# Pairwise bilinear interaction: x in a ring of five tiles, loads in pairs, four stores a tile, products in place

## The chip, the cores and the metric

One Trainium2 chip, one core of it. The time is microseconds of the device for one execution of the whole kernel. Engines: PE (matrix), DVE (vector), ACT (scalar), POOL (GpSimd), SP (issues transfers). Sixteen DMA engines move data between HBM and the on-chip buffer; transfers are issued here from the queues of SP, ACT and POOL.

## The reference

```python
# inputs: (4096, 32, 64) f32;  W: (496, 64, 64) f32
idx_i, idx_j = np.triu_indices(32, k=1)            # 496 pairs i < j
vidots = jnp.einsum('bpd,pde->bpe', inputs[:, idx_i, :], W)
y = vidots * inputs[:, idx_j, :]                   # (4096, 496, 64) f32
```

For each row b of the batch and each pair (i, j), the 64 numbers of field i are multiplied by the pair's own 64 x 64 matrix, and the result is multiplied element by element with field j. x is 33.6 MB, W 8.1 MB and the output 520.1 MB.

## The kernel before, in words

The 4096 rows are 16 blocks of 256; a block is two tiles of 128 rows (row 2p + k of a block is partition p of its tile k), so there are 32 tiles. Field i of a tile has a run of pairs (i, i+1) to (i, 31), which begins at pair p0[i]; the runs get shorter, from 31 pairs to 1.

**Weights.** W comes in four chunks of rows (`cuts`, `wrows`). Each is loaded with a pair per partition (`load_w`, L133), put in another order by a copy (`order_w`, L139, into a buffer of `tpool`), transposed by PE in eight blocks (`turn_w`, L148) and copied from PSUM to its place in wT (L151). A chunk takes four such rounds. The first chunk is done before the main loop; the rounds of the other three are placed at steps of the main loop by the lists `orders` and `turns`.

**x.** A block is loaded into one of two buffers of `xpool` (`new_x`, `load_x`, L81). For each run of 8 fields of a tile, PE transposes four pairs of fields (`turn_x`, L159) and ACT copies the result to an xT buffer in three pieces (L163 to L165; four buffers, `xtpool`). This is done AHEAD = 6 steps before the first use.

**Steps.** A step is one field i and up to 16 of its pairs. PE multiplies into one of four PSUM buffers (L259, one matmul for each half of the 64 outputs). Then either DVE multiplies the PSUM result with x_j into the output buffer `ot` (L279); or, for the first 16 pairs of i = 1, 3, ..., 13 (`aside`), ACT copies PSUM out (L276) and POOL multiplies (L277). In the first three tiles ACT copies straight into `ot` and POOL works in place; in later tiles ACT's copy goes to a `tmp` buffer of `tpool`.

**Stores.** The 496 pairs of a tile are divided by `bounds` into five groups of 90 to 105 pairs. Each group fills one of three `ot` buffers (`opool`) and is stored by one transfer from SP (L284); the very first group is stored in two parts. A row of a group, 23,040 to 26,880 bytes, is contiguous in HBM, so a store is 128 packets, eight for each DMA engine.

**Order.** The first three tiles (`LEAD`) go through the groups together: group 0 of tiles 0, 1, 2, then group 1, and so on, while the weights are still being prepared. After that it is tile by tile. Blocks 0 and 1 and the weights are loaded by SP at the start. Later blocks are loaded one at a time while the block before is used: blk + 1 is issued at step LATE = 6 of the first tile of blk (block 2 at that step of tile 3). Blocks 2, 3, 4, 6, 8, 10 and 12 are issued from ACT's queue, as one transfer of 16 KB a partition. Blocks 5, 7, 9, 11, 13, 14 and 15 (`fifteen`) are issued from POOL's queue (`load_fifteen`): 120 partitions over fifteen of the DMA engines, so that one is skipped; a tiny transfer (`turn_engines`, L97) that moves on the engine at which POOL's next transfer begins; and the 8 partitions left over in two transfers, each with half of the fields of both tiles, in packets of 4 KB (L105). In SBUF these blocks have a gap of 16 numbers between their two tiles.

The scheduler of the tile framework adds the semaphores. The order on an engine is the order in the program, and a pool's buffer is reused when its readers are done.

Of the kernel before, what the change touches and what calls it, by code (L numbers as in the profile page):

```python
# [8 lines left out]
F32 = mybir.dt.float32  # L9
# [3 lines left out]
def kernel(  # L13
# [15 lines left out]

    nc = tc.nc  # L30

    B, F, D = x.shape
    P = 128
    NB = 2
    assert 2 * D == P and B % (NB * P) == 0
    NBLK = B // (NB * P)
    NP = F * (F - 1) // 2
    E2 = D // 2
    BANK = 512
    CH = BANK // E2  # L40
    RUN = 8
    p0 = [i * (F - 1) - i * (i - 1) // 2 for i in range(F)]


    bounds = [0, p0[3], p0[6] + CH, p0[11], p0[17], NP]
    groups = list(zip(bounds[:-1], bounds[1:]))
    cap = max(b - a for a, b in groups)

    aside = (1, 3, 5, 7, 9, 11, 13)

    cuts = [0, P, 2 * P, NP - P, NP]
    wrows = list(zip(cuts[:-1], cuts[1:]))

    const = ctx.enter_context(tc.tile_pool(name="const", bufs=1))
    xpool = ctx.enter_context(tc.tile_pool(name="xpool", bufs=2))
    xtpool = ctx.enter_context(tc.tile_pool(name="xtpool", bufs=4))
    tpool = ctx.enter_context(tc.tile_pool(name="tpool", bufs=4))
    opool = ctx.enter_context(tc.tile_pool(name="opool", bufs=3))
    psum = ctx.enter_context(tc.tile_pool(name="psum", bufs=4, space=bass.MemoryType.PSUM))

    ident = const.tile([P, P], F32, tag="ident", name="ident")
    make_identity(nc, ident)

    xs = {}
# [4 lines left out]


    fifteen = (5, 7, 9, 11, 13, 14, 15)

    def new_x(blk: int):
        gap = 16 if blk in fifteen else 0
        wide = xpool.tile([P, NB * (F * D + 16)], F32, tag="xs", name=f"xs_{blk}")
        wide = wide[:, : NB * (F * D + gap)].rearrange("p (k n) -> p k n", k=NB)
        xs[blk] = wide[:, :, : F * D].rearrange("p k (f d) -> p k f d", d=D)

    def load_x(blk: int, eng, k0: int = 0, k1: int = NB):
        src = rows_of(x, blk).rearrange("(p k) f d -> p k f d", k=NB)  # L80
        eng.dma_start(out=xs[blk][:, k0:k1], in_=src[:, k0:k1])  # L81
# [4 lines left out]
    SWR = 120  # L86
# [13 lines left out]
    def load_fifteen(blk: int):  # L100
        rows = rows_of(x, blk).rearrange("(p k) f d -> p k f d", k=NB)
        dst = xs[blk]

        def part(ps: slice, fs: slice):
            tc.keep_in_program_order(nc.gpsimd.dma_start(out=dst[ps, :, fs, :], in_=rows[ps, :, fs, :]))  # L105

        part(slice(0, SWR), slice(0, F))
        turn_engines(1)
        for h in range(2):
            part(slice(SWR, P), slice(h * F // 2, (h + 1) * F // 2))  # L110


    wflat = w.rearrange("p d e -> p (d e)")
    raw, wT = {}, {}
    EU = 2 * BANK // P
    NU = E2 // EU


    def home_of(c: int, r: int):
        home, tag, n = (wrows[3][0], "w3", P) if c == 3 else (0, "w", 3 * P)  # L120
        if home not in wT:
            wT[home] = const.tile([P, n, E2], F32, tag=tag, name=f"wT_{home}")
        return wT[home][:, wrows[c][0] - home : wrows[c][0] - home + r, :]

    def load_w(c: int):

        a = wrows[c][0]
        if c == 2:
            raw[c] = home_of(c, P).rearrange("p r e -> p (r e)")
        else:  # L130
            pool, tag = (const, "w3") if c == 3 else (opool, "ot")
            raw[c] = pool.tile([P, D * D], F32, tag=tag, name=f"raw_{c}")
        nc.sync.dma_start(out=raw[c], in_=wflat[a : a + P])  # L133

    def order_w(c: int, k: int, copy):
        r = wrows[c][1] - wrows[c][0]
        rp = tpool.tile([P, EU, 2, D], F32, tag="tmp", name=f"rp_{c}_{k}")
        src = raw[c][:r, :].rearrange("p (d h e) -> p e h d", h=2, d=D)
        ins = copy(rp[:r], src[:, k * EU : (k + 1) * EU])  # L139
        if c > 0:  # L140
            tc.keep_in_program_order(ins)
        return rp

    def turn_w(c: int, k: int, rp, copy):
        r = wrows[c][1] - wrows[c][0]
        pt = psum.tile([P, EU, P], F32, tag="ps", name=f"ptw_{c}_{k}")
        for n in range(EU):
            nc.tensor.transpose(  # L148
                pt[:, n, :r], rp[:r, n].rearrange("p h d -> p (h d)"), ident[:r, :r]
            )  # L150
        copy(home_of(c, r)[:, :, k * EU : (k + 1) * EU], pt[:, :, :r].rearrange("p e r -> p r e"))  # L151

    def turn_x(blk: int, k: int, q: int, copy):


        pt = psum.tile([P, RUN // 2, P], F32, tag="ps", name=f"ptx_{blk}_{k}_{q}")
        for u in range(RUN // 2):
            f = q * RUN + 2 * u
            nc.tensor.transpose(  # L159
                pt[:, u, :], xs[blk][:, k, f : f + 2, :].rearrange("p f d -> p (f d)"), ident  # L160
            )
        xT = xtpool.tile([P, 2, RUN // 2, P], F32, tag="xT", name=f"xT_{blk}_{k}_{q}")
        copy(xT[:, 0], pt)  # L163
        copy(xT[D:, 1], pt[:D])  # L164
        copy(xT[:D, 1], pt[D:])  # L165
        return xT


    steps = [
        (g, i, c0, min(CH, F - 1 - i - c0))  # L170
        for i in range(F - 1)
        for c0 in range(0, F - 1 - i, CH)
        for g, (a, b) in enumerate(groups)
        if a <= p0[i] + c0 < b
    ]
    NS = len(steps)
    first = {}
    for s, (_, i, _, _) in enumerate(steps):
        first.setdefault(i, s)

    LEAD = 3
    NT = NBLK * NB
    sched = [
        (t, s) for g in range(len(groups)) for t in range(LEAD) for s in range(NS) if steps[s][0] == g
    ]
    sched += [(t, s) for t in range(LEAD, NT) for s in range(NS)]
    place = {ts: n for n, ts in enumerate(sched)}


    AHEAD = 6
    due: dict = {}
    for t in range(NT):
        for q in range(F // RUN):
            at = place[t, first[q * RUN]] - AHEAD
            due.setdefault(max(0, at), []).append(("x", t // NB, t % NB, q))
    for c, orders, turns in (
        (1, (2, 4, 8, 10), (4, 7, 12, 15)),
        (2, (16, 18, 25, 27), (30, 33, 36, 39)),  # L200
        (3, (46, 48, 50, 52), (56, 59, 62, 65)),
    ):
        for k in range(NU):
            due.setdefault(orders[k], []).append(("order", c, k))
            due.setdefault(turns[k], []).append(("turn", c, k))
    LATE = 6
    loads = {place[blk * NB, LATE]: blk + 1 for blk in range(2, NBLK - 1)}
    loads[place[LEAD, LATE]] = 2

    new_x(0)  # L210
# [4 lines left out]
    new_x(1)  # L215
# [5 lines left out]
    v, p, a = nc.vector.tensor_copy, nc.gpsimd.tensor_copy, nc.scalar.copy  # L221
    xT, rps = {}, {}
    xT[0, 0, 0] = turn_x(0, 0, 0, a)
    due[0] = [d for d in due[0] if d != ("x", 0, 0, 0)]
# [5 lines left out]
    ots = {}  # L230
    for s, (t, st) in enumerate(sched):
        blk, kt = divmod(t, NB)
        g, i, c0, m = steps[st]
        if s in loads:
            new_x(loads[s])
            if loads[s] in fifteen:
                load_fifteen(loads[s])
            else:
                load_x(loads[s], nc.scalar)
        for what, *args in due.get(s, ()):  # L240
# [4 lines left out]
            else:  # L245
                c, k = args
                rps[c, k] = order_w(c, k, ((v, v, p, v), (v, v, p, a))[k % 2][c])

        base, end = groups[g]
        pa = p0[i] + c0  # L250
        if pa == base:
            ots[t] = opool.tile([P, cap, D], F32, tag="ot", name=f"ot_{t}_{g}")
        ot = ots[t]
        ps = psum.tile([P, 2, CH, E2], F32, tag="ps", name=f"ps_{s}")
        for lo, hi in ((0, wrows[3][0]), wrows[3]):
            home, lo, hi = lo, max(pa, lo), min(pa + m, hi)
            if lo < hi:
                for h in range(2):
                    nc.tensor.matmul(  # L259
                        ps[:, h, lo - pa : hi - pa, :],  # L260
                        xT[blk, kt, i // RUN][h * D : (h + 1) * D, (i + h) % 2, i % RUN // 2, :],
                        wT[home][h * D : (h + 1) * D, lo - home : hi - home, :],
                        start=True,
                        stop=True,
                    )
# [4 lines left out]
        xj = xs[blk][:, kt, j : j + m, :].rearrange("p m (h e) -> p m h e", h=2)  # L270
        if i in aside and c0 == 0:

            tmp = dst
            if t >= LEAD:
                tmp = tpool.tile([P, CH, 2, E2], F32, tag="tmp", name=f"tmp_{s}")
            nc.scalar.copy(tmp, src)  # L276
            nc.gpsimd.tensor_mul(dst, tmp, xj)  # L277
        else:
            nc.vector.tensor_mul(dst, src, xj)  # L279

        ends = (p0[2], end) if s < NS and (t, g) == (0, 0) else (end,)
# [34 lines left out]
```

## Time and profile before

| | us |
|---|---|
| five executions, median (lowest to highest) | 1334.17 (1332.33 to 1335.5) |
| the profiled execution, its own time | 1335.4 |
| its span, first to last instruction | 1333.6 |
| PE busy, modelled | 1129.5 (85%) |
| DVE busy | 950.8 (71%) |
| POOL busy | 558.4 (42%) |
| ACT busy | 471.6 (35%) |
| DMA, mean of 16 engines | 9 tenths or more in all but one of 40 slices |
| TensorE clock granted | 0.956 |

How to read it: busy times are sums over the span for each engine, and they overlap. The page lists DMA queues with packets, bytes and the share of the sixteen DMA engines' time that their packets took; the records behind it have the start, size and duration of each packet. A wait "A <- B" is idle time of A that ended with B. A stretch is a window of the span with the busy time of each engine in it, the share of DMA time and GB/s.

### The profile page before, as it was taken

What the parts mean: (1) busy time and instruction counts of PE and PEld (TensorE: products, weight loads), DVE (VectorE), ACT (ScalarE), POOL (GpSimd) and SP (SyncE); (2) the same over time, 40 slices, a digit from 0 to 9 for tenths busy, and PEclk for the clock granted to TensorE, in tenths of its full rate; (3) what the DMA queues carried; (4) which work ended last, traced back from release to release, by engine and by line L of the source; (5) the groups of instructions that cost most, each with busy time, mean ns of one, the idle gap of its engine ahead of it and who ended that gap; (6) DMA issues with size and microseconds to landing.
All of it is one profiled execution on the core that took longest, in us unless ns stands there. A gap on an engine that the chain in (4) does not pass through costs nothing.

```text
span 1333.6 us, 16690 instructions
## 1 busy us (share of the span) xinstructions
PE 1129.5 (85%) x6656; PEld 599.2 (45%) x6656; DVE 950.8 (71%) x1258; ACT 471.6 (35%) x627; POOL 558.4 (42%) x264
## 2 busy tenths in 40 slices
PE   6989879878888888888888888898897988978894
PEld 3555434434444444444444444444444444434442
DVE  5878767767777776777767777676875767757784
ACT  4463323333333333233333333332333333333331
POOL 1752424444433445333453334542445443444441
PEclk9999999989999899999998989998998989989997
DMA  9999999999999999999999999999999999999998
GB/s 389 431 424 421 430 422 431 427 431 427 413 428 425 432 431 414 428 427 431 431 412 431 424 431 422 414 431 424 432 427 411 428 413 428 429 419 420 421 427 351
DMA packets 28143, 563.13 MB, mean 422 GB/s; under 512 B 3761, under 2 KB 3761, under 8 KB 4113
## 3 DMA queue, kind: packets, MB, share of 16 engines
q1 hardware_dynamic: 24192, 532.69, 94.0%
q0 software_dynamic: 2864, 14.70, 2.8%
q10 hardware_dynamic: 1008, 14.68, 2.6%
q8 instruction: 52, 0.85, 0.2%
q14 instruction: 27, 0.21, 0.0%
HBM read 41.94 MB, written 520.09 MB: 421 GB/s over the span
## 4 chain that ended last, share of the span: by engine, by line
DMA 61%; PE 16%; DVE 15%; POOL 3%; issue 2%; ACT 1%; DVEq 0%; SPq 0%; POOLq 0%; ACTq 0%
DMA out_dram<-ot 60%; PE ps L259 15%; DVE ot L279 14%; POOL ot L277 3%; PE ptx L159 1%; DMA xs<-in_r_inputs_dram 1%; DVE rp L139 0%; ACT tmp L276 0%; PE ptw L148 0%; DVEq L279 0%; POOL rp L139 0%; ACT ot L276 0%; SPq L133 0%; ACT xT L165 0%; ACT xT L163 0%
## 5 line engine op out<-in xcount | busy, mean ns | idle before, releaser
L279 DVE TENSOR_TENSOR ot<-ps,xs 128x1024 f32<-128x1024 f32 (+15 forms) x1248 | 935.9, 807 | 353.5 <-DMA out_dram<-ot 219.0
L259 PE MATMUL ps<-wT,xT 64*128 64x512 f32 (+12 forms) x6016 | 1039.6, 485 | 171.0 <-DVE ot L279 166.3
L259 PEld LDWEIGHTS ps<-wT,xT 64*128 64x128 f32 x6016 | 530.4, 194 | 620.9 <-DVE ot L279 384.2
L277 POOL TENSOR_TENSOR ot<-tmp,xs 128x1024 f32<-128x1024 f32 x203 | 479.2, 2361 | 697.6 <-ACT tmp L276 517.7
L276 ACT COPY tmp<-ps 128x1024 f32<-128x1024 f32 x203 | 205.5, 1012 | 471.6 <-PE ps L259 427.5
L163 ACT COPY xT<-ptx 128x512 f32<-128x512 f32 x128 | 75.0, 586 | 324.9 <-PE ptx L159 324.9
L159 PE MATMUL ptx<-ident,xs 128*128 128x128 f32 x512 | 84.4, 288 | 10.7 <-DMA xs<-in_r_inputs_dram 7.2
L159 PEld LDWEIGHTS ptx<-ident,xs 128*128 128x128 f32 x512 | 53.9, 141 | 82.8 <-DVE ot L279 58.0
L165 ACT COPY xT<-ptx 64x512 f32<-64x512 f32 x128 | 74.5, 582 | 1.6
L164 ACT COPY xT<-ptx 64x512 f32<-64x512 f32 x128 | 73.9, 577 | 1.5
L277 POOL TENSOR_TENSOR ot<-ot,xs 128x1024 f32<-128x1024 f32 x21 | 49.8, 2376 | 50.9 <-ACT ot L276 50.8
L276 ACT COPY ot<-ps 128x1024 f32<-128x1024 f32 x21 | 21.3, 1013 | 24.7 <-PE ps L259 15.0
L148 PE MATMUL ptw<-ident,rp 128*128 128x128 f32 (+1 forms) x128 | 17.7, 289 | 5.8 <-DVE rp L139 5.8
L139 DVE COPY rp<-raw 128x1024 f32<-128x1024 f32 x9 | 14.7, 1649 | 10.7 <-DMA raw<-in_L_rec_W_dram 10.7
L148 PEld LDWEIGHTS ptw<-ident,rp 128*128 128x128 f32 (+1 forms) x128 | 14.9, 150 | 13.8 <-DVE rp L139 5.2
L151 ACT COPY wT<-ptw 128x1024 f32<-128x1024 f32 (+1 forms) x15 | 14.8, 985 | 11.6 <-PE ptw L148 10.2
L105 POOL DMA_DIRECT2D xs<-in_r_inputs_dram x21 | 13.4, 637 | 0.0
L97 POOL DMA_DIRECT2D scratch<-in_r_inputs_dram x9 | 8.2, 911 | 0.3 <-issue 0.3
L139 POOL COPY rp<-wT 112x1024 f32<-112x1024 f32 x4 | 7.9, 1978 | 0.0
L139 ACT COPY rp<-raw 128x1024 f32<-128x1024 f32 x3 | 6.0, 1986 | 1.9 <-DMA raw<-in_L_rec_W_dram 1.9
L151 DVE COPY wT<-ptw 128x1024 f32<-128x1024 f32 x1 | 1.2, 1225 | 2.4 <-PE ptw L148 2.4
L163 ACT ACT_TABLE_LOAD x1 | 1.3, 1283 | 0.7 <-PEq L303 0.7
(6 smaller groups left out, 0.9 us busy)
## 6 DMA issues: line engine op xcount, KB each, us to landing
out_dram<-ot SPq DMA_DIRECT2D x64, 3360.0 KB, 16.3
out_dram<-ot SPq DMA_DIRECT2D x32, 3168.0 KB, 15.7
out_dram<-ot SPq DMA_DIRECT2D x32, 3104.0 KB, 17.0
out_dram<-ot SPq DMA_DIRECT2D x31, 2880.0 KB, 17.2
xs<-in_r_inputs_dram ACTq DMA_DIRECT2D x7, 2048.0 KB, 18.7
xs<-in_r_inputs_dram POOLq DMA_DIRECT2D x7, 1920.0 KB, 24.9
raw<-in_L_rec_W_dram SPq DMA_DIRECT2D x3, 2048.0 KB, 13.9
xs<-in_r_inputs_dram SPq DMA_DIRECT2D x2, 1024.0 KB, 10.4
```

The costliest lines, as they stand in the source:

```text
L105: tc.keep_in_program_order(nc.gpsimd.dma_start(out=dst[ps, :, fs, :], in_=rows[ps, :, fs, :]))
L139: ins = copy(rp[:r], src[:, k * EU : (k + 1) * EU])
L148: nc.tensor.transpose(pt[:, n, :r], rp[:r, n].rearrange("p h d -> p (h d)"), ident[:r, :r])
L151: copy(home_of(c, r)[:, :, k * EU : (k + 1) * EU], pt[:, :, :r].rearrange("p e r -> p r e"))
L159: nc.tensor.transpose(pt[:, u, :], xs[blk][:, k, f : f + 2, :].rearrange("p f d -> p (f d)"), ident)
L163: copy(xT[:, 0], pt)
L164: copy(xT[D:, 1], pt[:D])
L165: copy(xT[:D, 1], pt[D:])
L259: nc.tensor.matmul(ps[:, h, lo - pa : hi - pa, :], xT[blk, kt, i // RUN][h * D : (h + 1) * D, (i + h) % 2, i % RUN // 2, :], wT[home][h * ...
L276: nc.scalar.copy(tmp, src)
L277: nc.gpsimd.tensor_mul(dst, tmp, xj)
L279: nc.vector.tensor_mul(dst, src, xj)
```

## The change

- x lives in one buffer `xb` of five tile slots with gaps. A pair of blocks (four tiles) is loaded at once, at step LATE = 4 of the last tile of the pair before, into the four slots that are not in use: the even block from ACT's queue, the odd block from POOL's queue by `load_fifteen`. So blocks 3, 5, 7, 9, 11, 13 and 15 skip a DMA engine. Where the second block's slots are 0 and 1, its two tiles are used in reverse order.
- The 8 partitions left over are divided by tile: two transfers with packets of 8 KB.
- After the first three tiles a tile has four groups, of 118, 125, 127 and 126 pairs (30,208 to 32,512 bytes a row), and the chunk of i = 15 is divided in 10 + 6. The first three tiles have six groups of 72 to 91 pairs. All output buffers lie in one tile `ob`.
- ACT always copies into the output buffer and POOL multiplies in place; `tpool` is gone.
- xT has two buffers in later tiles. In the first three tiles two more lie in slot 0 of `xb`.
- wT is one tile. The chunks are now 112, 128, 128, 128 rows; a chunk's raw rows lie where the next chunk's transposed rows will be, the last one's at the end of `ob`, and the reordered copies lie in `ob`. The step lists for chunks 2 and 3 are different. A step no longer has its matmuls divided at the border between weight tiles.

```diff
+    LEAD = 3
+    lead = [0, p0[3], p0[6], p0[9], p0[13], p0[18], NP]
+    later = [0, p0[4], p0[9], p0[15] + 10, NP]
-    bounds = [0, p0[3], p0[6] + CH, p0[11], p0[17], NP]
-    cuts = [0, P, 2 * P, NP - P, NP]
+    cuts = [0, NP - 3 * P, NP - 2 * P, NP - P, NP]
...
-    xpool = ctx.enter_context(tc.tile_pool(name="xpool", bufs=2))
-    xtpool = ctx.enter_context(tc.tile_pool(name="xtpool", bufs=4))
-    tpool = ctx.enter_context(tc.tile_pool(name="tpool", bufs=4))
-    opool = ctx.enter_context(tc.tile_pool(name="opool", bufs=3))
+    wT = const.tile([P, NP, E2], F32, tag="wT", name="wT")
+    xb = const.tile([P, 5 * FD + 3 * GAP], F32, tag="xb", name="xb")
+    xtb = const.tile([P, 2 * XT], F32, tag="xtb", name="xtb")
+    ob = const.tile([P, 3 * cap1, D], F32, tag="ob", name="ob")
+    def out_home(n: int, later_: bool):
+        o, c = ((2 - n % 3) * cap1, cap1) if later_ else ((2 - n % 3) * cap0, cap0)
+        return ob[:, o : o + c, :]
+    starts = [0, FD + GAP, 2 * FD + GAP, 3 * FD + GAP, 4 * FD + 2 * GAP]
+    def slot_of(blk: int):
+        e, second = divmod(blk, 2)
+        return ((1, 3), (2, 0))[e % 2][second]
+    def tile_of(t: int):
+        blk, k = divmod(t, NB)
+        return blk, 1 - k if slot_of(blk) == 0 else k
...
         part(slice(0, SWR), slice(0, F))
         turn_engines(1)
-        for h in range(2):
-            part(slice(SWR, P), slice(h * F // 2, (h + 1) * F // 2))
+        for k in range(NB):
+            part(slice(SWR, P), slice(k, k + 1))
...
-        (2, (16, 18, 25, 27), (30, 33, 36, 39)),
-        (3, (46, 48, 50, 52), (56, 59, 62, 65)),
+        (2, (16, 18, 26, 29), (24, 27, 32, 36)),
+        (3, (56, 58, 66, 72), (62, 68, 74, 78)),
...
-    LATE = 6
-    loads = {place[blk * NB, LATE]: blk + 1 for blk in range(2, NBLK - 1)}
-    loads[place[LEAD, LATE]] = 2
+    LATE = 4
+    loads = {place[2 * NB * e - 1, LATE]: 2 * e for e in range(1, NBLK // 2)}
...
-            new_x(loads[s])
-            if loads[s] in fifteen:
-                load_fifteen(loads[s])
-            else:
-                load_x(loads[s], nc.scalar)
+            tc.keep_in_program_order(load_x(loads[s], nc.scalar))
+            load_fifteen(loads[s] + 1)
...
-            tmp = dst
-            if t >= LEAD:
-                tmp = tpool.tile([P, CH, 2, E2], F32, tag="tmp", name=f"tmp_{s}")
-            nc.scalar.copy(tmp, src)
-            nc.gpsimd.tensor_mul(dst, tmp, xj)
+            nc.scalar.copy(dst, src)
+            nc.gpsimd.tensor_mul(dst, dst, xj)
```

## The prediction

> **What bounds the kernel now.** I read the page's DMA queues first, because the page's DMA row is at 9 tenths in every slice while no engine is near that.
>
> ```profile
> q1 hardware_dynamic: 24192, 532.69, 94.0%
> q0 software_dynamic: 2864, 14.70, 2.8%
> q10 hardware_dynamic: 1008, 14.68, 2.6%
> q8 instruction: 52, 0.85, 0.2%
> HBM read 41.94 MB, written 520.09 MB: 421 GB/s over the span
> ```
>
> Columns: packets, MB, share of the time of 16 DMA engines. The shares add up to 99.6%: the transfers alone fill the span. SP's queue (q1, the stores) is 94.0%. So only a shorter, better packed or better balanced set of transfers can make this kernel faster; an engine matters only where it hands over a store too late.
>
> Second, the waits, for who follows whom.
>
> ```profile
> DVE ot L279 <- DMA out_dram<-ot: 219.0, 104, 5.8
> POOL ot L277 <- DMA out_dram<-ot: 160.4, 64, 4.9
> PE ptx L159 <- DMA xs<-in_r_inputs_dram: 7.2, 2, 5.9
> ```
>
> DVE and POOL wait for output buffers to be stored: arithmetic follows the stores. PE waits for x only twice, at the start, so the x loads come early enough.
>
> Third, the packet records of the trace. The median packet takes 855, 921, 940 and 996 ns for 23,040, 24,832, 25,344 and 26,880 bytes: (996 - 855) / 3,840 bytes = 0.0367 ns a byte, and 9 ns a packet are left; a 4-byte completion mark also takes 9 ns. By this rate all packets need 1,308.3 us on each engine; their recorded durations add up to 1,328.7. The 20.4 us between are stalls inside packets. The span is 1,333.6.
>
> Fourth, stretches of 35 us, to see where those stalls are: around an x load issued by ACT, around one by POOL, with none, and the end.
>
> ```profile
> 424.00:459.00 35.00, 28.05 (x152) 14.84 (x148) 21.37 (x26) 11.68 (x15) 16.54 (x7) 0.90 1.00 424
> 512.00:547.00 35.00, 28.71 (x174) 15.27 (x172) 23.58 (x34) 12.31 (x18) 16.59 (x10) 0.95 1.00 414
> 460.00:495.00 35.00, 30.75 (x190) 16.33 (x192) 26.33 (x38) 12.33 (x16) 16.00 (x7) 1.00 1.00 430
> 1320.00:1333.60 13.60, 0.00 (x0) 0.00 (x0) 0.00 (x0) 0.00 (x0) 0.00 (x0) 0.50 0.53 228
> ```
>
> The last columns are the share of time the DMA engines are busy, and GB/s. All are busy throughout, yet move less when x is loaded. Over all seven windows of a kind the means are 424.4 (ACT) and 414.0 (POOL); thirteen without a load have 430.2. So an ACT load loses 35 x (1 - 424.4/430.2) = 0.47 us and a POOL load 1.32 us, and the fourteen together 7 x 1.79 = 12.5 us. In the packet records the loss sits at a load's start: about ten store packets there take 1.5 to 1.9 us in place of 1.0. In the last stretch the engines are idle for half the time: of the last store's sixteen marks the median lands at 1,327.4 us and the last at 1,332.7. One DMA engine trails by 5.2 us, and it sets the end.
>
> **The change part by part.**
>
> *Fewer, larger stores.* Before: 32 tiles x 5 + 1 = 161 stores. After: three tiles of 6, one store more in the first, and 29 tiles of 4: 135. Each of the 26 saved is 128 row packets and 16 marks of 9 ns: 26 x 144 x 9 ns / 16 = 2.1 us. Bytes are unchanged. Nothing hides this, since it is time of the bounding engines; SP's 26 saved issues are hidden behind its waits for DVE (1,221 us). I take -2.1. Two stores of 26,880 bytes a row land 7.95 us apart (306.47 and 314.42 us) and 8 x 0.996 us = 7.97, so a store has no further fixed price here.
> The Trainium skill ("DMA: Bandwidth & Descriptors", "Anatomy of one DMA") fits about 2.0 us of fixed time to every DMA issued from GpSimd; carried over to these stores it would make 26 x 2.0 = 52 us, an estimate by that page, which the spacing of 7.95 us contradicts for queued stores.
>
> *Two x blocks together.* Seven ACT loads and seven POOL loads stay, with the same bytes; they now start together in seven places. Now a pair costs 0.5 + 1.3 = 1.8 us. Bounds: if the start's stall is paid once for both and only packet prices remain it could go to about 0.2 us (-11 us in all); if two reading queues disturb each other it could double to 3.6 (+12.5). The nearest row is the POOL window, one episode of reading: 1.3 if ACT's part vanishes in it, 1.8 if not. I take the middle: 7 x 0.24 = -1.7 us.
> The Trainium skill (same page, "Rules for kernel authors") says that spreading DMAs over issuing engines for bandwidth does not help, since all run on the same 16 engines. The 99.6% agrees; by the rule alone this term is 0 and the forecast 1.7 us higher.
>
> *Are the loads in time?* They are issued at step 4 of 47 in the pair's last tile; the next tile's transposes stand 6 steps before its end. With a store packet of 32 KB (9 ns + 0.0367 x 32,256 = 1.19 us), one of ACT (0.61) and one of POOL (0.31) taking turns, ACT's eight packets an engine need 8 x 2.1 = 17 us, some 3 us after the issue. The compute between is 37/47 of a tile; a tile computes in 35.4 us (stores ready 7.05 us after their buffer is free for 99 of 496 pairs), so 28 us: 8 us spare. POOL's block is wanted two tiles later. ACT's trigger also waits for DVE and POOL to leave the slots; behind it stand a PSUM copy and x^T copies, which PE needs; DVE is at most a few steps of 0.8 us behind, and the spare covers it: 0.
>
> *The eight leftover rows by tile.* 224 packets of 4 KB become 112 of 8 KB: 112 x 9 ns / 16 = 0.06 us: 0.
>
> *Products in place, one large output tile.* ACT's copy now waits for the output slot, not for a spare buffer; POOL's product has 2,376 ns in place and 2,361 otherwise, 203 x 15 ns = 3 us on an engine 42% busy. Queued behind ACT's wait are the x^T copies, with PE behind them. PE has only four PSUM buffers in rotation, so it stops at DVE's wait for the slot anyway; only the group that begins with i = 9 meets ACT first. The built program has 926 semaphore instructions on DVE, before 297: 629 at 0.05 us (the chain's DVE queue pieces) = 31 us, 1 us a tile. The x^T ring shrinks from four to two, but each refill follows PE's last reader in PE's own order. All of it lies beside the stores: a tile computes in 35.4 us and is stored and loaded in 1,333.6/32 = 41.7. I take 0; without this cover it would be 1 to 2 us a tile.
>
> *Slack of the ring.* A store is issued 1.1 to 8 us before the one ahead of it has landed, once only 0.6 (at 90 us, where the DMA engines are idle for 0.55 us). Three buffers give twice the store time minus the compute time minus the trailing: 2 x 7.8 - 7.2 = 8.4 us before, 2 x 9.4 - 9 = 9.8 after: a little better. In the first three tiles it is worse: 2 x 6.3 - 6.3 = 6.3 us with stores of 80 pairs, and each of the weight's twelve later turning steps costs about 0.6 us of compute (693 pairs took 54.3 us from 43.6 to 97.9 us, 49.5 at the later rate, with eight such steps). Four of them now fall into two or three stores: 2.4 us against 6.3, minus 2 us of trailing. Bounds: -0.6 (the present hole closes) to +4; I take 0.
>
> *The trailing engine.* The slowest sixteenth of the undisturbed store packets is about 43 ns over the median at 23,040 bytes as at 26,880: flat in size, so it looks like a price a packet. On one engine, 208 fewer packets would be 9 us less, and it would no longer trail. If the price goes with bytes nothing changes. The part POOL loads skip one engine seven times before and after. Bounds: -5.2 (no trailing) and +3 (the larger ring lets it trail further). I take -2.
>
> Sum: -2.1 - 1.7 - 2 = -5.8 us: span 1,333.6 - 5.8 = 1,327.8. The profiled execution has 1,335.4 us with 1.8 outside its span, 1.2 over the median of the five runs, 1,334.2; on that median I forecast 1,328.4.
>
> **The rivals.**
>
> *More is gained (1,322).* Both the trailing and most start stalls go: -2.1 - 5.2 - 5 = -12. For it: the flat 43 ns, and stalls only at starts. Against it: POOL's descriptors begin later than ACT's, so a pair still has two starts.
>
> *The pairing changes nothing (1,332).* Starts stall as before, the trailing stays: -2.1. For it: the engines are the same sixteen; the skipped engine is relieved as often as before.
>
> *Two readers disturb each other (1,344), the other side.* The place is the 30 us after each pair's issue, where stores, ACT's and POOL's packets alternate. Price: 1.79 us more a pair, 7 x 1.79 - 2.1 = +10.4. For it: a POOL load already loses over twice what an ACT load loses, and its packets stall with the stores. Against it: after the start the ACT windows run at nearly the free rate. It decides above 1.79 + 2.1/7 = 2.1 us a pair if the trailing stays, and reaches 0.2% above 2.5.
>
> *The first three tiles starve (1,338).* Smaller stores leave 6.3 us of slack, and weights and products share one buffer; if stores come 8 us late there in all, that is +8 - 4. For it: the hole at 90 us. Against it: the weight steps are spread over more of the stretch.
>
> **How the numbers follow.** A measurement of this kernel tells about 0.2%, 2.7 us, from no change: 1,331.5 to 1,336.9 is "the same". Chances: the forecast 0.45 (1,325 to 1,331), more gained 0.20, nothing from pairing 0.19 (the same), readers disturbing 0.09 and starving 0.07 (slower). Faster 0.65, same 0.19, slower 0.16. The range reaches from a full gain to the upper edge of "nothing" and the milder starving: 1,320 to 1,338.
>
> **What would show it.** q1 falls to about 20,450 packets with the same MB; seven stretches near 415 GB/s for pairs, the rest near 431; the last store's marks closer than 5.2 us; the waits for out_dram<-ob still on DVE, ACT and POOL; PE's wait for x still at the start alone. I am wrong if the stretches with pairs fall below 405 over 35 us, if DMA slices before 170 us fall below 9, or if the trailing grows past 6 us.

## The result and the profile after

The changed kernel takes 1,337.6 us, median of 22 runs (1,335.6 to 1,338.3), beside 1,334.4 of the kernel before: a ratio of 1.0022 [1.0016, 1.0028]. It is slower by 0.22%, where 0.4% faster was forecast, and lies just inside the upper end of the range. The profiled execution has a span of 1,335.8 us, 2.2 more than before.

The DMA queues of the changed kernel, from its page (packets, MB, share of the time of 16 DMA engines):

```profile
q1 hardware_dynamic: 20576, 532.69, 93.5%
q0 software_dynamic: 2640, 14.70, 2.8%
q10 hardware_dynamic: 1008, 14.68, 2.7%
HBM read 41.94 MB, written 520.09 MB: 421 GB/s over the span
```

The packets went as forecast: 26 stores fewer take 3,744 packets away, and x block 1 adds 128, since its place in the ring has a gap and its rows come in two pieces. By the rate of the prediction (9 ns a packet and 0.0367 ns a byte) all packets need 1,306.3 us on each engine, before 1,308.3. Their recorded durations are 1,326.3, before 1,328.7. So the transfers became 2.4 us shorter and the span 2.2 us longer: the DMA engines are idle for 9.5 us of it, before 4.9.

Stretches of 35 us of the changed kernel that begin with each pair of loads; then five without a load; then the end. The last columns are the DMA engines' busy share and GB/s:

```profile
146.00:181.00 35.00, 29.73 (x178) 16.67 (x176) 24.44 (x36) 12.28 (x18) 16.40 (x10) 0.90 0.99 402
300.00:335.00 35.00, 23.66 (x116) 12.25 (x112) 15.86 (x22) 8.76 (x12) 16.50 (x10) 0.76 1.01 422
465.00:500.00 35.00, 26.24 (x146) 13.56 (x142) 20.20 (x27) 10.82 (x15) 16.79 (x10) 0.85 1.00 415
627.00:662.00 35.00, 26.02 (x136) 13.73 (x134) 18.84 (x25) 10.74 (x15) 16.75 (x10) 0.85 1.00 416
791.00:826.00 35.00, 27.13 (x134) 14.22 (x130) 18.56 (x25) 10.30 (x14) 16.23 (x10) 0.80 0.99 408
956.00:991.00 35.00, 26.89 (x134) 13.93 (x132) 18.47 (x24) 10.30 (x14) 15.51 (x9) 0.80 1.01 416
1119.00:1154.00 35.00, 27.12 (x136) 13.90 (x132) 18.75 (x25) 10.65 (x15) 16.62 (x10) 0.80 0.99 402
...
545.00:580.00 35.00, 30.97 (x180) 16.23 (x176) 26.32 (x34) 13.16 (x18) 16.48 (x7) 0.95 1.00 430
710.00:745.00 35.00, 31.29 (x182) 15.89 (x180) 26.31 (x36) 13.08 (x19) 16.48 (x7) 0.95 1.01 432
875.00:910.00 35.00, 31.58 (x188) 16.24 (x186) 25.64 (x38) 13.06 (x18) 15.19 (x7) 0.95 1.00 428
912.00:947.00 35.00, 30.18 (x176) 15.64 (x172) 25.45 (x34) 12.90 (x18) 16.53 (x7) 0.95 0.95 408
1040.00:1075.00 35.00, 31.20 (x188) 16.22 (x186) 25.55 (x38) 13.06 (x18) 14.96 (x7) 0.95 0.99 427
...
1320.00:1335.80 15.80, 0.00 (x0) 0.00 (x0) 0.00 (x0) 0.00 (x0) 0.00 (x0) 0.50 0.42 180
```

The stretches with pairs have 411.6 GB/s on average. Against the 430.2 of before's stretches without a load a pair loses 35 x (1 - 411.6/430.2) = 1.5 us, where two separate loads lost 1.8: in these stretches the pairing gave the mean engine about what was forecast. Two signs say that the mean engine is not what matters. At 912 us no x is loaded, and yet the engines are busy for only 0.95 of the time. And at the end they are busy for 0.42 of 15.8 us; before it was 0.53 of 13.6.

The waits of the changed kernel for stores and for x (total us, times, longest):

```profile
DVE ob L313 <- DMA out_dram<-ob: 173.7, 77, 8.4
ACT ob L310 <- DMA out_dram<-ob: 126.3, 46, 10.4
...
PE ptx L200 <- DMA xb<-in_r_inputs_dram: 7.5, 2, 6.0
```

Compute still follows the stores, and PE waits for x at the start alone. What grew is the longest single wait for a store, to 10.4 us on ACT (5.8 on DVE before).

**One DMA engine is late.** The trace has the completion mark of each of the sixteen engines for each store. Of the last store's marks, fifteen come between 1,326.5 and 1,328.2 us and one at 1,334.7: 8.2 us after the median, 5.2 before. Two more readings from the marks are used below. First, *the lag*: how long a store's last mark comes after its median one. In the changed kernel it is 1.1 us at 265 us, 2.4 at 330, 4.2 at 606, 7.2 at 768, 7.9 at 1,095 and 9.1 at 1,297; from 768 us on each pair of loads takes 3.1 to 3.6 us of it away, and by the next pair it is back. Second, *the late engine's extra*: the advance of the last mark over 16 stores (20 with five stores a tile), which is four tiles and one pair of loads, less what the stores' own packets need by the rate. In a stretch without loads the last mark gains a recurring 0.2 to 0.4 us a store on that rate (at 710 us: 0.26, 0.33, 0.39, 0.31, 0.28, 0.31, 0.40) while the median one gains 0.1 in all of them together. That pattern is the same from store to store and from kernel to kernel: it is one engine whose stores run about 3.5% slower, and it is last where the pattern is seen. The packet records bear this out. An engine's next packet starts where its last one ends, so the late engine can be followed from packet to packet: from 1,150 to 1,296 us its store packets of 30,208, 32,000, 32,256 and 32,512 bytes take on average 47, 52, 30 and 41 ns more than the median packet of the same size. So nearly every packet is slower, and by an amount that does not simply rise with its size.

### The profile page after: what moved, and what is told of

Read it like the earlier page. It is cut to its first block, busy times and chain, and to the rows that moved or that the text cites. A ratio compares the mean times of both kernels' runs of the same rounds, so it can differ in the third digit from the quotient of the medians.

```text
span 1335.8 us, 17383 instructions
## 1 busy us (share of the span) xinstructions
PE 1151.8 (86%) x6644; PEld 604.2 (45%) x6644; DVE 952.1 (71%) x1287; ACT 471.6 (35%) x627; POOL 558.6 (42%) x264
## 4 chain that ended last, share of the span: by engine, by line
DMA 47%; PE 25%; DVE 10%; issue 10%; POOL 4%; ACT 3%; DVEq 0%; ACTq 0%; POOLq 0%; SPq 0%
DMA out_dram<-ob 46%; PE ps L297 22%; DVE ob L313 10%; POOL ob L311 3%; ACT ob L310 2%; PE ptx L200 2%; PE ptw L191 0%; DMA xb<-in_r_inputs_dram 0%; POOL xb L152 0%; POOL ob L181 0%; DVE ob L181 0%; POOL scratch L144 0%; ACT xtb L202 0%; ACT xtb L204 0%; ACT xtb L203 0%
## 5 line engine op out<-in xcount | busy, mean ns | idle before, releaser
L313 DVE TENSOR_TENSOR ob<-ps,xb 128x1024 f32<-128x1024 f32 (+4 forms) x1277 | 939.9, 792 | 350.1 <-DMA out_dram<-ob 173.7
L297 PE MATMUL ps<-wT,xtb 64*128 64x512 f32 (+15 forms) x5760 | 1019.4, 493 | 142.6 <-DVE ob L313 73.8
L311 POOL TENSOR_TENSOR ob<-ob,xb 128x1024 f32<-128x1024 f32 x224 | 529.2, 2367 | 747.0 <-ACT ob L310 719.1
L297 PEld LDWEIGHTS ps<-wT,xtb 64*128 64x128 f32 x5760 | 512.9, 196 | 614.9 <-DVE ob L313 250.0
L310 ACT COPY ob<-ps 128x1024 f32<-128x1024 f32 x224 | 226.8, 1013 | 488.5 <-PE ps L297 325.2
L202 ACT COPY xtb<-ptx 128x512 f32<-128x512 f32 x122 | 71.5, 586 | 311.2 <-PE ptx L200 311.2
L200 PE MATMUL ptx<-ident,xb 128*128 128x128 f32 x512 | 88.0, 297 | 11.1 <-DMA xb<-in_r_inputs_dram 7.5
L200 PEld LDWEIGHTS ptx<-ident,xb 128*128 128x128 f32 x512 | 56.3, 146 | 62.5 <-issue 34.7
L204 ACT COPY xtb<-ptx 64x512 f32<-64x512 f32 x122 | 71.0, 582 | 3.0
L203 ACT COPY xtb<-ptx 64x512 f32<-64x512 f32 x122 | 70.4, 577 | 2.9
L297 PE MATMUL ps<-wT,xb 64*128 64x512 f32 (+15 forms) x244 | 42.4, 465 | 3.4 <-DVE ob L313 1.5
## 6 DMA issues: line engine op xcount, KB each, us to landing
out_dram<-ob SPq DMA_DIRECT2D x3, 2912.0 KB, 12.7
```

Of the source, the lines that this page charges most:

```text
L200: nc.tensor.transpose(pt[:, u, :], x_tile(t)[:, f : f + 2, :].rearrange("p f d -> p (f d)"), ident)
L297: nc.tensor.matmul(ps[:, h, :m, :], xT[t, i // RUN][h * D : (h + 1) * D, (i + h) % 2, i % RUN // 2, :], wT[h * D : (h + 1) * D, pa : pa + ...
L310: nc.scalar.copy(dst, src)
L311: nc.gpsimd.tensor_mul(dst, dst, xj)
```

## The experiments

Each ratio is to the kernel before, measured beside it on the same chip. "The paired form" is the changed kernel.

**Pairing undone: `a2_unpaired`.** POOL's load is issued one tile after ACT's.

```diff
+    odd = {place[2 * NB * e, LATE]: 2 * e + 1 for e in range(1, NBLK // 2)}
...
-            load_fifteen(loads[s] + 1)
+        if s in odd:
+            load_fifteen(odd[s])
```

> The changed kernel with the pair taken apart: ACT's load of the even block stays at step 4 of the pair's last tile before, POOL's load of the odd block comes one tile later. Theory 'pairing': the collision goes (ACT's 16 KB packets from a mean of 646 ns back to 614, 1.8 us in all for each engine) and stretches with a load return to about 424 and 414 GB/s; the time falls by 1.5 to 2 us to about 1336. Theory 'leftover' and rival 'schedule': the stalls at the starts come back as separate ones, so the sum of stalls stays near 20 us an engine and the time within 1 us of 1337.6.

Measured: 1,333.36 us, ratio 0.9989 [0.9981, 0.9998]. Of the difference of 0.22% to before, all is gone with the pairing. But the recorded durations on the mean engine are 1,327.4 us, 1.1 more than in the paired form. The time is saved elsewhere: the last store's marks spread over 6 us and none stands apart, and the late engine's extra is 12.0 to 12.5 us per four tiles, where the paired form has 13.1 to 14.3 and the kernel before 12.0 to 12.8. Here the slow engine is the last one in parts of the run only; from 1,143 us on the last marks keep to the rate, without its pattern.

**One skip less: `a4_first_not_skipped`.** Block 3 is loaded by ACT over all sixteen engines.

```diff
-            load_fifteen(loads[s] + 1)
+            if loads[s] == 2:
+                tc.keep_in_program_order(load_x(3, nc.scalar))
+            else:
+                load_fifteen(loads[s] + 1)
```

> The changed kernel, but the first pair's odd block (block 3, issued at about 145 us) comes in one plain transfer from ACT over all sixteen engines, so that the trailing engine is not relieved there. Theory 'leftover' holds that every skip counts, as the trailing engine never idles: 16 packets of 8 KB more on it and 2 leftover ones less = 14 x 0.31 = 4.3 us: about 1342, spread of the last marks about 12 us. Rival 'schedule': the skip at 145 us is wasted, because that engine is not behind there and runs ahead into idleness: no change, 1337.6, spread 8.2.

Measured: 1,340.91 us, ratio 1.0046 [1.0034, 1.0059], 3.3 us over the paired form. A skip at 150 us, when the lag is still small, counts at the end.

**One skip more: `c1_eighth_skip`.** Block 14 is loaded by POOL too.

```diff
...
-    starts = [0, FD + GAP, 2 * FD + GAP, 3 * FD + GAP, 4 * FD + 2 * GAP]
+    starts = [0, FD + GAP, 2 * FD + GAP, 3 * FD + 2 * GAP, 4 * FD + 3 * GAP]
...
-            tc.keep_in_program_order(load_x(loads[s], nc.scalar))
+            if loads[s] == 14:
+                load_fifteen(14)
+            else:
+                tc.keep_in_program_order(load_x(loads[s], nc.scalar))
```

> Edit: in the changed kernel block 14 too is loaded by POOL with the fifteen-engine transfer (one skip more, at about 1,120 us); the slots get a gap each, so ACT's seven loads use 8 KB packets in four cases (+0.3 us). Theory 'one engine sets the end': in the changed kernel one engine ends 8.2 us after the median one, and a skip takes about 14 packets of 8 KB at 0.31 us, 4.3 us, from it; the others gain 0.3 us each. 1,337.6 - 4.3 + 0.6 = 1,334, and the last store's marks within 4 to 5 us. Rival 'all engines lose it in the pairs': no gain, and a POOL load costs 0.85 us more than an ACT load: 1,338 to 1,339, the last mark still 8 us behind. Rival 'two POOL loads in a row come too late': a wait of PE for xb near 1,140 us and more than 1,342.

Measured: 1,333.75 us, ratio 1.0000 [0.9991, 1.0009]. The lag is 8.4 us at 1,087 and 0.8 at 1,218, after the two POOL loads, and the last store's marks lie within 3.5 us. The mean engine works longer (recorded durations 1,329.7 us, 3.4 more than in the paired form), and the kernel is 0.2 to 0.3% faster than the paired form. A stretch after the extra skip, and the end, from a view of this kernel:

```profile
1250.00:1285.00 35.00, 32.01 (x198) 16.46 (x194) 26.49 (x37) 12.45 (x17) 14.94 (x7) 1.00 1.00 431
...
1320.00:1333.70 13.70, 0.00 (x0) 0.00 (x0) 0.00 (x0) 0.00 (x0) 0.00 (x0) 0.50 0.70 304
```

In the last 13.7 us the engines are busy for 0.70 of the time instead of 0.42 of 15.8: the idle end is what went.

**Another engine skipped: `c4_other_skipped`.** The first tiny transfer is one row longer, so that all seven loads skip the neighbour.

```diff
-    turn_engines(5)
+    turn_engines(6)
...
-    turn_engines(11)
+    turn_engines(10)
```

> Edit: in the changed kernel the first small transfer has six rows in place of five, so that the seven 120-partition loads skip the next engine. Theory 'one engine is slow in storing, by itself': it now gets all its POOL packets, 7 x 4.3 = 30 us more; the ring lets it trail about 10 us, then the other engines wait for it: about 1,337.6 + 25 to 30 = 1,363 to 1,368. Rival 'no engine is slow by itself; what is skipped trails, or the trailing comes with the pairs on any engine': 1,336 to 1,339.

Measured: 1,360.96 us, ratio 1.0205 [1.0192, 1.0219]. So it is one engine that is slow by itself, not whichever is skipped. The lag is 8.3 us at 330 us and from there to the end mostly between 7 and 10 (6.9 to 12.5): the others get no further ahead and stand still instead, since there are three output buffers and the late engine still holds one. Stretches without a load, from a view of this kernel:

```profile
425.00:460.00 35.00, 30.17 (x182) 15.36 (x182) 25.43 (x35) 12.34 (x17) 16.47 (x7) 1.00 0.96 411
720.00:755.00 35.00, 31.65 (x182) 16.03 (x182) 25.48 (x35) 12.35 (x17) 16.47 (x7) 0.95 0.96 411
880.00:915.00 35.00, 31.66 (x186) 16.46 (x184) 26.48 (x37) 13.31 (x18) 14.13 (x6) 0.95 0.98 420
```

These are the shares of 0.96 to 0.98 that the paired form shows only late (0.95 at 912 us). The recorded durations are 1,333.7 us of a span of 1,358.9, so the mean engine idles for 25 us.

**The same, unpaired: `d2_unpaired_other`.** The two edits together.

> Edit: the unpaired form with the neighbouring engine skipped in place of the slow one (the same edit on the paired form took 1,361.0). If the slow engine loses 1.3 us a pair because its stores are disturbed while both queues read, skipped or not, the unpaired form takes 7 x 1.3 = 9 us less: about 1,352. If the loss exists only for an engine that stores alone while the other fifteen read, it is the same as the paired one: 1,360 to 1,362.

Measured: 1,358.79 us, ratio 1.0188 [1.0175, 1.0201], 2.2 us under the paired one and far from 1,352. The late engine's extra is 16.3 us per four tiles (16.5 in the paired one). So pairing costs the slow engine hardly anything while it takes its share of POOL's load; it makes the *skip* worth less: 16.5 - 13.6 = 2.9 us paired, 16.3 - 12.3 = 4.0 unpaired.

**The leftover rows.** They were a second suspect, since the division by tile makes half as many packets of twice the size. `b1_left_by_tile` is the kernel before with that division alone; `c2_left_aside` is the paired form with a small transfer after each leftover transfer, meant to keep both off the skipped engine (its edit is the one shown); `a1_left_by_field` is the paired form with the old division.

```diff
             part(slice(SWR, P), slice(k, k + 1))
+            turn_engines(8)
```

> The kernel before with one part of the change alone: the leftover partitions by tile. Theory 'leftover': its skipped engine gets 2.1 us more; since another engine ended 2 us after the second slowest there (marks at 1330.2 and 1332.3 us), the end moves by 0 to 2 us: 1334.4 to 1336.5, and the leftover packets show on eight engines only. Rivals 'schedule' and 'pairing': no change, 1334.4.

> Edit: in the changed kernel a small transfer of eight rows follows each of the two leftover transfers, so that both leftover transfers fall on the same eight engines and none on the engine that the 120-partition transfer skips. Theory 'one engine sets the end': that engine is spared one 8 KB packet (0.31 us) in each of seven loads, 2.2 us, or two packets, 4.4 us, if it has had both: 1,333 to 1,335.5. Rival 'it does not set the end' or 'the leftover never fell there': 1,337 to 1,338.5.

> The changed kernel with one part undone: the 8 leftover partitions are loaded by halves of the fields again (packets of 4 KB), not by tile. Theory 'leftover': by tile, both leftover transfers fall on the same eight DMA engines, the trailing one among them, which so gets two packets of 8 KB in each of the seven skipping loads in place of two of 4 KB; undone, the trailing engine has 7 x 0.30 = 2.1 us less: the marks of the last store spread over about 6 us in place of 8.2, and the time falls from 1337.6 to about 1335.5 (ratio to the kernel before near 1.001). Rival 'schedule' (the skips come at the wrong times) and rival 'pairing' (two reading queues collide): no change, 1337.6, spread 8.2.

Measured: b1 1,335.09 us, 1.0005 [0.9996, 1.0013]; c2 1,338.07 us, 1.0031 [1.0019, 1.0043]. Neither moves the time by what can be measured here. But `c2` does not do what it was meant to: followed from packet to packet, the skipped engine carries two leftover packets of 8 KB (309 ns each) in each of the last four loads of the changed kernel, and two in each of the last four of `c2` as well. In the kernel before it carries two of 4 KB. So what the leftover costs the slow engine in the paired form, by these durations some 0.6 us a pair, was not tested. That the loss does not hang on it is shown by `a2` above, which has the same leftover and no loss. `a1` took 1,394.12 us (1.0443 [1.0429, 1.0457]) and tests something else. Its waits:

```profile
POOL xb L152 <- DVE ob L313: 112.1, 4, 28.3
POOL xb L152 <- DMA xb<-in_r_inputs_dram: 80.1, 3, 29.0
```

POOL stands still seven times, 27 us on average, before a leftover transfer, with its products queued behind. In the one buffer xb the regions of the two halves interleave; that the second transfer therefore waits for the first is the likely reading, and three of the seven waits are recorded so. The division by tile avoids this wait.

**Five stores a tile: `a3_five_stores`.** The old division into groups, the buffers as large as they were.

```diff
-    later = [0, p0[4], p0[9], p0[15] + 10, NP]
+    later = [0, p0[3], p0[6] + CH, p0[11], p0[17], NP]
...
-    cap1 = max(b - a for a, b in groups[LEAD])
+    cap1 = 127
```

> Edit: the changed kernel with the five stores a tile of the kernel before in its 29 later tiles (output buffers stay as large as they were); 29 stores more. By the packets, 29 x 144 x 9 ns / 16 = +2.3 us on every engine, the last one too: 1,340. If the slow engine pays about 40 ns for every packet, as the prediction supposed, 29 x 9 x 40 ns = 10 us more: about 1,347. If smaller stores keep the other engines closer to the slow one and nothing is lost by that, the last mark comes about 7 us after the median one in place of 8.2, at the same total.

Measured: 1,344.38 us (1,337.8 to 1,346.2, wider than any other), ratio 1.0072 [1.0055, 1.0088]: 6 to 7 us over the paired form, between the two expected figures. The marks say which of them holds without loads: there the slow engine gains 0.24 us a store of about 25 KB a packet (2.2 us in 67.4), with four stores 0.33 us a store of 32 KB (2.3 us in 65.6). So over whole tiles the extra goes with the bytes and not with the number of packets (size by size it is uneven, as shown above). 2.3 us of the difference are packets; the extra per four tiles is 13.9 us on average and up to 14.8, in place of 13.6, which makes 2 us more in seven pairs. The rest, about 2 us, stays open. The last mark comes 6.9 us after the median one, as was expected if smaller stores keep the others closer to the slow one.

**Where POOL's load falls.** `d1_half_tile_later` issues it at step 28 of the same tile. It loses as much as the paired form, and it had been measured on another chip than the unpaired form, so both were run again on one chip, with the changed kernel itself; then a tile and a half, `f1_tile_and_half`.

```diff
-    odd = {place[2 * NB * e, LATE]: 2 * e + 1 for e in range(1, NBLK // 2)}
+    odd = {place[2 * NB * e - 1, 28]: 2 * e + 1 for e in range(1, NBLK // 2)}   # d1, e2
+    odd = {place[2 * NB * e, 28]: 2 * e + 1 for e in range(1, NBLK // 2)}       # f1
```

> Edit: in the changed kernel POOL's load is issued at step 28 of 47 of the tile in which ACT's is issued at step 4, about 21 us later in place of together (the unpaired form, 42 us later, took 1,333.4). Theory 'the two readers at once cost it': ACT's packets are through some 17 to 20 us after the issue, so nearly the whole gain is back: 1,333 to 1,335. Rival 'it is the distance in time of the relief, or the change of tile': half or nothing of it, 1,335.5 to 1,338.

> The changed kernel as it is, once more, on the chip of the next three. If its loss does not depend on the chip, 0.2% slower than before, about 1,337; if it does, within 0.1% of before or beyond 0.4%.

> The unpaired form, unchanged, on the same chip. Theory 'pairing costs the slow engine 4 us': 1,333 to 1,334, some 4 us under the changed kernel beside it. Rival 'the two were on different chips': level with it.

> POOL's load half a tile after ACT's, unchanged, on the same chip. If two readers at once cost the time, it is level with the unpaired form; if it depends on where in the tile POOL's load falls, level with the changed kernel or slower (1,337 to 1,339).

> Edit: in the unpaired form POOL's load is issued at step 28 of 47 of the next tile, a tile and a half after ACT's, in place of step 4. In the unpaired form the slow engine's work over the store rate was 12.0 to 12.8 us per four tiles in most, in the paired and the half-tile form 13 to 14.3. If the distance from ACT's load decides (a tile or more is good): 12 to 12.8 us and 1,333 to 1,334.5. If the place in the tile decides (step 28 is bad): 13 us and more, 1,337 to 1,339.

| POOL's load after ACT's by | ratio | late engine's extra per four tiles, mean |
|---|---|---|
| 0 (after; e0) | 1.0022 [1.0016, 1.0028]; 1.0028 [1.0019, 1.0038] | 13.6; 13.6 us |
| half a tile (d1; e2) | 1.0033 [1.0021, 1.0045]; 1.0034 [1.0021, 1.0047] | 13.4; 13.5 |
| a tile (a2; e1) | 0.9989 [0.9981, 0.9998]; 0.9999 [0.9991, 1.0008] | 12.3; 12.4 |
| a tile and a half (f1) | 1.0004 [0.9996, 1.0013] | 12.7 |
| two tiles (the kernel before) | 1 | 12.2 |

The extra is read where the slow engine is last. Single periods overlap (11.0 to 13.5 us in e1, 12.6 to 14.4 in d1); the means do not.

The chip is not it: e0 repeats the loss. Two loads in flight at once are not it either: half a tile later ACT's packets are through (1,121 to 1,137 us in one case, POOL's 1,155 to 1,185) and the loss is whole. Nor is it the place in the tile, since step 28 of the next tile is nearly as good as step 4. A distance of a tile or more is what the good forms have in common. Where the skipped engine can be followed from packet to packet by their start and end times, the difference lies inside POOL's load: there 7 to 13 of its store packets take 0.1 to 0.5 us longer than the rate. All its store packets in one such load together exceed the rate by 2.9 to 3.6 us at zero (seven loads of two runs), 3.0 to 4.1 at half a tile (ten loads), 2.6 and 2.9 at a tile and a half (two loads) and 2.3 to 2.8 at a tile (seven loads). Why the distance does this was not found.

**Two skips' worth: `c3_unpaired_eighth`.** Unpaired, and block 14 by POOL as well.

> Edit: the changed kernel with POOL's load one tile after ACT's (the unpaired form, 1,333.4 measured) and block 14 loaded by POOL as well. In the unpaired form no engine ends more than 3 us after the next. Theory 'one engine sets the end': the trailing engine is nearly level there, the skip can give 1 to 3 us and costs 0.6: 1,331 to 1,333.5. Rival: no engine trails and only the price remains: 1,334.

Measured: 1,334.33 us, ratio 1.0010 [1.0000, 1.0019]. Where the slow engine is not late, one skip more gains nothing and has its price. Beside c1 on the same chip it also shows that paired and unpaired are alike once the slow engine has been relieved enough.

**ACT's loads in the stores' own queue.** `d3_unpaired_sp`, `e3_paired_sp` and `f2_tile_and_half_sp` are the unpaired form, the paired one and f1, each with this edit:

```diff
-            tc.keep_in_program_order(load_x(loads[s], nc.scalar))
+            tc.keep_in_program_order(load_x(loads[s], nc.sync))
```

> Edit: the unpaired form with the seven ACT loads issued by SP, so that they stand in the stores' own queue. If the 0.47 us that an ACT load loses at its start comes from two queues taking turns, 7 x 0.47 = 3.3 us go: 1,330. If it is the price of reading, the same 1,333.4. If SP then waits for the x slots and holds back stores, more than 1,336, with the wait on SP's line.

> Edit: the changed kernel, paired, with ACT's seven loads issued by SP instead, so that they stand in the stores' own queue. If ACT's queue taking turns with the stores while POOL's load begins is what costs the slow engine, this is level with the unpaired form or better: 1,331 to 1,334. If pairing costs by POOL's load and the block's arrival alone, 1,336 to 1,338. If SP waits for the slots and holds back stores, 1,340 and more.

> Edit: the same, with ACT's loads issued by SP as in the fastest form so far (1,331.7). If the distance decides: 1,331 to 1,332. If the place in the tile decides: 1,335 to 1,337.

Measured: d3 1,331.69 us, 0.9983 [0.9975, 0.9992], the fastest form of all; its recorded durations are 1,326.3 us, 1.1 less than the unpaired form's. e3 took 1,353.74 us, 1.0149 [1.0136, 1.0162], and f2 1,335.24 us, 1.0007 [0.9998, 1.0016]. Two stretches of e3 with a pair of loads:

```profile
300.00:335.00 35.00, 21.16 (x120) 10.69 (x116) 15.00 (x20) 11.15 (x15) 17.10 (x11) 0.89 1.00 375
463.00:498.00 35.00, 26.12 (x142) 13.07 (x138) 19.13 (x24) 12.32 (x16) 19.31 (x11) 0.90 1.00 366
```

The engines are busy throughout and move 375 and 366 GB/s, 4.5 and 5.2 us lost in these two pairs: recorded durations of 1,348.8 us, 22.5 more than in the paired form. Here the two loads disturb each other on every engine, as the rival of the prediction had it for the paired form. The wait on SP that was expected for that case is not there: SP waits 5.3 us for slots in all. So what is best for one form (SP's queue) is worst for the other.

## Why the prediction was wrong

*Fewer, larger stores, -2.1:* right. The recorded durations fell by 2.4 us with stalls nearly the same (20.0 us, before 20.4).

*Two x blocks together, -1.7:* right for the mean engine by the stretches (1.5 us a pair; the forecast's middle was 1.55); in the packet records the stalls fell by only 0.4 us over the whole run, and against the unpaired form the durations are 1.1 us less. It was the wrong engine to sum over. On the slow engine a pair costs 13.6 - 12.2 = 1.4 us more, some 9 us in six to seven pairs; how this divides between the lag at the end and the waiting of the others was not worked out. The records shown for this term were means over sixteen engines; the part of the loss that lands on one engine is a sixteenth in them.

*The trailing engine, -2:* this is the step that failed, and with it the sign. The trailing was to shrink by 2 us; it grew from 5.2 to 8.2 us, +3.0, the far end of the bounds given. Two readings were wrong. "Flat in size, so it looks like a price a packet": the slow engine's extra is 3% to 3.5% of its store time with five stores a tile as with four, so 208 fewer packets gave it 208 x 9 ns and no more. And "one DMA engine trails by 5.2 us, and it sets the end", taken together with the slowest sixteenth of the packets, put two engines into one: after 1,200 us the last marks of the kernel before keep to the rate, without the slow engine's pattern. There three of the seven skips come late and close together (blocks 13, 14 and 15, at 1,004, 1,087 and 1,169 us), and from about 1,040 us on the slow engine is no longer the last one; that these skips bring it level is read from the trace and was not tested. The changed kernel has one skip every 164 us, the last at 1,124. This spacing alone is not what costs: `a2` has the same spacing, one tile later, and no loss. What the runs show in place of the -2 is that a skip is worth less to the slow engine when the load follows ACT's at once, 2.9 us in place of 4.0, so that it falls behind. "Skips one engine seven times before and after" counted the skips and did not weigh them.

The Trainium skill ("DMA: Bandwidth & Descriptors", "Latency and other measured facts") says that two of the sixteen DMA engines are usually slower in traces, and gives as its best guess contention at the descriptor rings of transfers issued from GpSimd. The first half agrees with what the marks show of one engine. The guess does not cover it: the 0.2 to 0.4 us a store are there in stretches of 80 us in which POOL has no transfer in flight. Which numbers the engines here have, no run shows. The same page's rule that was weighed in the prediction, that spreading transfers over issuing engines does not help ("Rules for kernel authors"), is too short for d3 and e3: the total bytes an engine moves are the same, but against the same form with ACT's queue SP's gave about -0.1% in one case and +1.2% in the other.

*Loads in time, products in place, ring, first three tiles, 0 each:* right. PE waits for x at the start alone; POOL's products have 2.36 us in place; DVE's extra semaphores show no wait; the engines are idle for about 1 us at 130 to 145 us, within the bounds given. One sum among these is off: the ring's slack of 8.4 us before and 9.8 after leaves out the trailing that its own formula takes away. With it, it is 8.4 - 5.2 = 3.2 us and 9.8 - 8.2 = 1.6 us, an estimate by which the ring is a little tighter at the end and not a little better.

*The rivals.* "Two readers disturb each other" was on the right side for a reason that did not hold: the price is 1.5 us a pair on the mean engine, below the 1.79 that it started from. Of the signs named beforehand, "the trailing grows past 6 us" came true, and two of seven pair stretches fell to 402, under the 405 named, at a mean of 411.6.

The sum as it came: the last store's median mark went from 1,327.4 to 1,326.6 us (-0.9) and the lag from 5.2 to 8.2 (+3.0): +2.1 of the 2.2 us of the span. c1 and c4 show that the lag is a cause: relieved once more, the engine costs nothing and the loss to before is gone; not relieved at all, it costs another 23 us.

## What to carry to other kernels

Where transfers fill the span, look at the last DMA engine and not at the mean of sixteen: the completion marks of each store, last against median, followed from store to store, show whether one engine falls behind and when. A schedule that gives such an engine relief is a budget per period: here an extra of about 12 us per four tiles left no loss and 13.6 did. An edit that leaves the count of relieving transfers alone can still spoil it by where it puts them. A difference among packets has to be followed on one engine before it is called a price a packet.

## What had not been expected

- One DMA engine stores 3% to 3.5% slower than its neighbours, also when nothing is loaded (0.2 to 0.4 us a store of 8 packets), on each of the five chips that the experiments ran on.
- While fifteen engines read x for POOL, store packets of the sixteenth, which has only two leftover packets of that load, take 0.1 to 0.5 us longer each, 2.3 to 4.1 us a load where it can be followed; it is less where ACT's load came at least a tile earlier.
- The same ACT block in SP's queue gives the fastest form when POOL's load is a tile away (0.9983, hardly clear of the 0.9989 and 0.9999 with ACT's queue) and costs 16 us when it is issued together with it (1,353.7 against 1,337.6).
